# A separate VectorE side queue for layer 1's additions, served first

## The chip, the cores and the metric

The kernel runs on one core of a Trainium2 chip. The core has five engines that run their own instruction streams and meet at semaphores: PE (TensorE, matrix products), DVE (VectorE), ACT (ScalarE), POOL (GpSimd, here mostly an issuer of DMAs) and SP (SyncE, issues DMAs only). SBUF is the working memory, PSUM the small memory that PE writes its products to. The metric is the device time of one execution in microseconds (us). Several executions are timed and the median is given. The profile is one further execution, recorded by the hardware profiler.

## The reference

The input is x with 8 images of 32 channels and 128 x 128 pixels, in float32. Two layers follow each other, each adding its result to its input.

```
# layer 0: x = x + conv0(gn(x)), gn = group norm with 16 groups
xb   = patch_match_stack(g)          # per pixel the 8 best of 25 shifts, 32 -> 256 channels
dct  = conv(xb, dct_w, groups=32)
h    = relu(dw3x3(conv1x1(xb, w1), w2))
h    = relu(dw3x3(conv1x1(h,  w3), w4))
wien = sigmoid(dw3x3(conv1x1(h, w5), w6))
x    = x + conv1x1(conv(wien * dct, inv_dct_w, groups=32), agg_w)
# layer 1: x = x + conv1(gn(x)), one 5x5 kernel for every channel
x    = x + conv2d_5x5(gn(x), kernel, padding=2)
```

`patch_match_stack` sums squared differences between x and its 25 shifts over the channels, sums them over 3 x 3 pixels, takes the 8 smallest of the 25 for each pixel and gathers the shifted pixels.

## The kernel before

**The main loop.** Layer 0 of an image is worked off in steps of 8 rows: 16 steps and one for the edge, 17 per image, 136 in all, and two more to drain the pipeline. In each step the loop `for i in (3, 2, 1, 0)` makes four turns. Turns 3, 2 and 1 work on the three pairs of 1x1 and depthwise 3x3 convolutions, each for another row group, and turn 0 on the last multiplication and aggregation. So a row group that leaves stage 1 in one step enters stage 2 in the next. The 256 channels of each stage are split in two. The depthwise convolution of the first 128 channels runs on PE (L751, evicted by ACT at L764), that of the second 128 on DVE as eight multiply-adds over 128 x 1024 elements (L725, after a first tap by ACT at L722; the activation at L729 is ACT's too). The 1x1 products of PE are L670 (second half, evicted by ACT at L678) and L694 (first half, evicted by ACT at L701). L631 gathers pixels as a product with a selection matrix, which ACT makes at L616 and L617. In turn 0, PE makes L810 (`pc`), DVE multiplies it into the accumulators (L818), PE aggregates (L831, `pa`), and DVE adds the layer's input and takes statistics (L839, L840).

**Side work.** All that isn't in this pipeline is written as generators that say with `yield` on which queue they go on: "D" for DVE with a cost in us, "A" for DMAs and ACT, "P" and "Q" for PE. On D there are the squared differences of the next image (L444), their box sums (L508 to L520), the eight best (L536, L537), the places to gather from (L551 to L560) and layer 1 of the image that layer 0 has just finished. `push` (L211) lets a generator run to its next `yield` and appends it to that queue. `run` (L217) takes tasks from the front of a queue as long as the taken costs stay under a credit. In each turn, `tick` (L1017) serves D once: it adds a share of the image's side work to `owed` and gives `run("D", ...)` that credit. P is served before L810 in each turn, after L670 of the turn and after the L831 left over from the step before (`next(later)`); A is served once per turn, later. PE, DVE and ACT execute their instructions in the order in which the program wrote them, which these queues set.

**Layer 1** of an image works in four blocks of eight channels. `load` (L873) reads 8 channels from DRAM on POOL's queue. Then on D, DVE normalises them (L897, eight operations). On P, PE multiplies by the five bands of the 5x5 kernel (L924, `p5` in the program and `p` in the profile's names: 20 products into two PSUM tiles). On D again, DVE adds the two PSUM tiles to x (L936, two additions), POOL issues four DMAs of the result (L938), and the load of the next block goes to A. Four rows in the middle of the image that the two halves of the partitions can't reach are done by `middle` (L948: L959, L960 and 25 multiply-adds at L972). For the last image the additions carry a cost of 3.6 and include the next block's normalisation.

**PSUM.** The pool `ps_x` has five tiles, used by L631, L670, L694, L810, L831, L924 and others. A tile can be written again when its reader is through. The tiles of L924 are held until the additions at L936 have read them.

The text numbers layer 1's blocks of an image 0 to 3. "Image 0" is the first whose layer 1 runs, which is while layer 0 works on the next image.

Of the kernel before, what the change touches and what calls it, by code (L numbers as in the profile page):

```python
# [16 lines left out]
P = 128  # L17
# [27 lines left out]
def bm3d_conv_preact(  # L45
# [155 lines left out]

    queues = {"D": deque(), "A": deque(), "P": deque(), "Q": deque()}

    PAIR = 1.95
    pairs = [0]
# [3 lines left out]
    def push(task):  # L211
        want = next(task, None)
        if want:
            which, cost, *wait = want
            queues[which].append((cost, task, now[0] + (wait[0] if wait else 0)))

    def run(which, credit=1e9, limit=2):  # L217

        q, took = queues[which], 0.0
        for _ in range(len(q) if which != "D" else 1000):  # L220

            i = next(
                (
                    i
                    for i, (c, _, at) in enumerate(q)
                    if at <= now[0] and (c != PAIR or pairs[0] < limit)
                ),
                None,
            )
            if i is None or took >= credit:  # L230
                break
            cost, task, _ = q[i]
            del q[i]
            took += cost
            pairs[0] += cost == PAIR
            push(task)
        if which == "Q":
            pairs[0] = 0
        return took
# [8 lines left out]
    def group_stats(mv, name):  # L248

        lhsT = cst[:, C_G : C_G + P]  # L250
        mr = work.tile([P, 2], F32, name=f"mr_{name}", tag="mr")
        tmp = work.tile([P, 2], F32, name=f"tmp_{name}", tag="stmp")
        yield "P", 0
        pm = ps_x.tile([P, 512], F32, name=f"pm_{name}", tag="x")
        nc.tensor.matmul(pm[:, 0:1], lhsT, mv[:, 0:1], start=True, stop=True)
        nc.scalar.copy(mr[:, 0:1], pm[:, 0:1])
        yield "D", 0.3
        nc.vector.tensor_sub(tmp[:, 0:1], mv[:, 0:1], mr[:, 0:1])
        nc.vector.scalar_tensor_tensor(
            tmp[:, 1:2], tmp[:, 0:1], tmp[:, 0:1], mv[:, 1:2], op0=ALU.mult, op1=ALU.add  # L260
        )
        yield "P", 0
        pv = ps_x.tile([P, 512], F32, name=f"pv_{name}", tag="x")
        nc.tensor.matmul(pv[:, 0:1], lhsT, tmp[:, 1:2], start=True, stop=True)
        nc.scalar.copy(tmp[:, 0:1], pv[:, 0:1])
        yield "D", 0.2
        yield from inverse_std(mr[:, 1:2], tmp[:, 0:1], tmp[:, 0:1])
        return mr
# [579 lines left out]
    def layer1(b):  # L848

        yield "D", 0.2  # L850
        mv = work.tile([P, 2], F32, name=f"mv1_{b}", tag="mv1")
        nc.vector.bn_aggr(mv, stats[b].rearrange("p a b -> p (a b)"))
        mr = yield from group_stats(mv, f"b{b}")
        dg = work.tile([C, 2, C], F32, name=f"dg_{b}", tag="dg")
        for i in range(2):
            nc.vector.tensor_scalar(
                dg[:, i], ident[:C, :C], mr[:C, i : i + 1], None, op0=ALU.mult
            )
        yield "P", 0
        pb = ps_x.tile([P, 512], F32, name=f"pb_{b}", tag="x")  # L860
        nc.tensor.matmul(
            pb[:, : 2 * C], ones, dg.rearrange("p a b -> p (a b)"), start=True, stop=True
        )
        bc = work.tile([P, 2, C], F32, name=f"bc_{b}", tag="bc")
        nc.scalar.copy(bc.rearrange("p a b -> p (a b)"), pb[:, : 2 * C])
        last = b == NB - 1
        if last:
            ends = xnp.tile([P, HR, HX], F32, name="ends", tag="xn")
            ends = ends.rearrange("p r x -> p (r x)")[:, : 8 * 4 * W]
            ends = ends.rearrange("p (g c x) -> p g c x", g=8, x=W)  # L870
        xys = {}

        def load(c):  # L873


            if last:
                m = work.tile([P, 2, 4, W], F32, name=f"xo_{c}", tag="sel", bufs=4)
                t = [ends[:, c // 4], ends[:, c // 4 + 1], m[:, 0], m[:, 1]]
            else:
                t = [  # L880
                    work.tile([P, 4, W], F32, name=f"{name}_{b}_{c}_{e}", tag=name)
                    for name, e in (("xy", 0), ("xm", 0), ("xy", 1), ("xm", 1))
                ]
            src = x1d[b].rearrange("c y x -> y c x")
            nc.gpsimd.dma_start(t[0], src[:, c : c + 4])
            for h in range(2):
                nc.gpsimd.dma_start(
                    t[1][64 * h : 64 * h + 64], src[64 - 64 * h : P - 64 * h, c + 4 : c + 8]
                )
            nc.gpsimd.dma_start(t[2], src[:, c + 4 : c + 8])  # L890
            xys[c] = t

        def normalise(c):
            t = xys[c]
            for e in range(2):
                for i in range(4):
                    nc.vector.tensor_scalar(  # L897
                        t[3 - 2 * e][:, i],
                        t[e][:, i],
                        bc[:, 0, c + 4 * e + i : c + 4 * e + i + 1],  # L900
                        bc[:, 1, c + 4 * e + i : c + 4 * e + i + 1],
                        op0=ALU.subtract,
                        op1=ALU.mult,
                    )

        for c in range(0, C if last else 8, 8):
            load(c)
        push(middle(b, mr))
        for c in range(0, C, 8):
            if c == 0 or not last:  # L910
                yield "D", 2.0, 1 if last else 3
                normalise(c)
            yield "P", 0
            ps = [
                ps_x.tile([P, 4, W], F32, name=f"p5_{b}_{c}_{e}", tag="x") for e in range(2)
            ]
            t = xys.pop(c)

            for k, dx in enumerate((0, -2, -1, 1, 2)):
                xa, xz = max(0, -dx), min(W, W - dx)  # L920
                for h in range(2):
                    for e in range(2):
                        r, o = 64 * h, 64 * ((h + e) % 2)
                        nc.tensor.matmul(  # L924
                            ps[e][o : o + 64, :, xa:xz],
                            band[r : r + 64, dx + 2, r : r + 64],
                            t[3 - 2 * e][r : r + 64, :, xa + dx : xz + dx],
                            start=k == 0,
                            stop=k == 4,
                        )  # L930
            yield "D", 3.6 if last else 1.6
            if last and c + 8 < C:
                normalise(c + 8)
            for e in range(2):
                y = t[2 * e]
                nc.vector.tensor_add(y, y, ps[e])  # L936
                for a, z in ((0, 62), (66, P)):
                    nc.gpsimd.dma_start(  # L938
                        out[b, c + 4 * e : c + 4 * e + 4, a:z].rearrange("c y x -> y c x"),
                        y[a:z],  # L940
                    )
            if c + 8 < C and not last:
                yield "A", 0, 1
                load(c + 8)

        done.add((b, 0))
# [62 lines left out]
    def end(b, n, xr, j0, j1):  # L1009
        yield from final_add(b, n, accs.pop((3, b, n)), xr, j0, j1)  # L1010
        if n == NS:
            push(layer1(b))

    total = 5.5 + 3.3 + 36 * 1.95 + 4 * 4.6 + 32 * 1.85 + 4 * 2.6 + 4 * 3.6 + 6.6
    owed = [0.0]

    def tick(b, i):  # L1017

        now[0] += 1
        owed[0] += total / (NS - 2 if b else NS - 6) * (0.4 if i == 0 else 0.2)  # L1020
        owed[0] -= run("D", owed[0], 2 if i else 0) if owed[0] > 0 else 0
        owed[0] = min(owed[0], 6.0)

    def turn(credit):
        now[0] += 1
        run("D", credit)
        run("A")
        run("P")
        run("Q")

    def until(cond, credit):
        while not cond():
            turn(credit)

    with tc.manual_schedule(engines=ORDERED):
# [6 lines left out]
        for u in range(7):  # L1042
            unit(gather_load, u)

            for _ in range({2: 3, 3: 1}.get(u, 0)):
                turn(4.0)
            unit(gather_select, u - 2)
            unit(gather_pixels, u - 3)
# [6 lines left out]
        for s in range(len(steps) + 2):  # L1055
# [10 lines left out]
            for i in (3, 2, 1, 0):  # L1066
# [22 lines left out]
                if s < len(steps):  # L1089
                    unit(gather_select, u + 1, (0,))  # L1090
                    unit(gather_load, u + 3)
                    tick(b, i)
# [85 lines left out]
```

## Time and profile before

| | us |
|---|---|
| median of 3 runs | 6544.47 (6539.76 to 6554.23) |
| the profiled execution's own time | 6544.27 |
| its span, first to last instruction | 6542.5 |
| PE busy | 6179.8 (94%) |
| DVE busy | 5857.8 (90%) |
| ACT busy | 5058.6 (77%) |
| POOL busy | 3087.2 (47%) |
| layer 1's additions (L936) | 64 of 680 ns each |
| layer 1's products (L924) | 4.48 us for a block's 20 |

A row of the waits says which instruction stood idle until which other was through, with the total in us, how often, and the longest. A row of a timeline gives the start, the length, the engine, the line, what is written from what, and in brackets how long the engine was idle before and who released it. The mean clock granted to TensorE is 0.98 of full speed. Each DMA's issue is a row of its queue's engine.

### The profile page before, as it was taken

The numbers are of one execution on the slowest core, as the hardware profiler recorded it, in microseconds if no ns is written. First come the engines' busy times: TensorE is split into PE (matmuls) and PEld (weight loads), VectorE is DVE, ScalarE is ACT, GpSimd is POOL, SyncE is SP. The second block draws the span as 40 slices with busy tenths as digits, with TensorE's granted clock in tenths as the row PEclk, the third lists the DMA queues.
The fourth block names the chain that finished last, engine by engine and source line by source line (L and its number), as shares of the span: only waits on it lengthen the run. The fifth ranks groups of instructions, "written<-read, shape, count | busy, mean of one in ns | idle before, by whom it ended". The sixth has DMA issues, their size and how long they took to land.

```text
span 6542.5 us, 234200 instructions
## 1 busy us (share of the span) xinstructions
PE 6179.8 (94%) x102306; PEld 3215.9 (49%) x102306; DVE 5857.8 (90%) x8828; ACT 5058.6 (77%) x6698; POOL 3087.2 (47%) x5015
## 2 busy tenths in 40 slices
PE   4799999999999999999999999999999999999997
PEld 1444445455554545545454544544545454455553
DVE  7899988999989999999989999889998999878776
ACT  5787769778787877887788787977869788787772
POOL 8345436444364444644446444554345544334334
PEclk8899999999999999999999999999999999999998
DMA  4555555555555555565556555555555555455553
GB/s 85 126 134 144 125 126 143 141 143 138 131 149 138 137 146 129 145 151 134 140 132 156 136 137 141 134 142 140 139 135 134 146 146 138 115 147 144 136 134 81
DMA packets 544960, 886.21 MB, mean 135 GB/s; under 512 B 248880, under 2 KB 312944, under 8 KB 543936
## 3 DMA queue, kind: packets, MB, share of 16 engines
q0 software_dynamic: 383648, 611.87, 37.3%
q1 hardware_dynamic: 157776, 258.11, 16.1%
q8 instruction: 805, 13.19, 0.9%
q10 hardware_dynamic: 2512, 1.25, 0.1%
q14 instruction: 219, 1.79, 0.1%
HBM read 420.60 MB, written 216.49 MB: 97 GB/s over the span
## 4 chain that ended last, share of the span: by engine, by line
PE 55%; DVE 26%; POOL 5%; ACT 5%; DMA 4%; issue 4%; SPq 0%; ACTq 0%; DVEq 0%; POOLq 0%
PE pw L751 18%; DVE acc L725 17%; PE pv L670 14%; PE p L694 13%; PE pg L631 4%; POOL xtd L424 3%; DVE idx L537 3%; PE pc L810 2%; DMA t<-t 2%; DVE df L444 1%; PE pd L459 1%; PE p L924 1%; PE pa L831 1%; DVE acc L818 1%; ACT df L452 1%
## 5 line engine op out<-in xcount | busy, mean ns | idle before, releaser
L725 DVE SCALAR_TENSOR_TENSOR acc<-tv,dwv,acc 128x1024 f32<-128x1024 f32 (+3 forms) x3264 | 4032.1, 1237 | 163.7 <-ACT acc L722 59.9
L751 PE MATMUL pw<-t,dwd 96*32 96x254 f32 (+7 forms) x31680 | 2113.2, 419 | 23.8 <-DMA t<-t 17.9
L751 PEld LDWEIGHTS pw<-t,dwd 96*32 96x32 f32 (+1 forms) x31680 | 1079.9, 110 | 850.1 <-issue 385.5
L616 ACT ACTIVATE sel<-ib,nplace 128x1024 f32<-128x1024 uint8 x1024 | 1170.6, 1143 | 62.3 <-DMA ib<-idxd 62.3
L617 ACT ACTIVATE sel<-sel 128x1024 f32<-128x1024 f32 x1024 | 1086.0, 1061 | 32.5
L670 PE MATMUL pv<-acc,lw 128*32 128x512 f32 x8448 | 964.3, 593 | 49.9 <-DVE acc L818 41.7
L694 PE MATMUL p<-acc,lw 128*32 128x256 f32 x16768 | 977.4, 380 | 19.4 <-DVE xy L936 19.4
L602 POOL DMA_DIRECT2D ib<-idxd x512 | 293.0, 572 | 1209.2 <-ACT sel L616 1099.4
L791 POOL DMA_DIRECT2D xf<-xbd x1088 | 653.6, 633 | 329.2 <-PE pc L810 187.1
L694 PEld LDWEIGHTS p<-acc,lw 128*32 128x32 f32 x16768 | 568.0, 111 | 411.2 <-issue 59.3
L678 ACT COPY tv<-pv 128x512 f32<-128x512 f32 (+2 forms) x784 | 437.0, 578 | 366.9 <-PE pv L670 358.8
L729 ACT ACTIVATE acc<-acc 128x1024 f32<-128x1024 f32 (+3 forms) x408 | 417.3, 1023 | 349.0 <-DVE acc L725 348.8
L631 PE MATMUL pg<-sel,xt 120*32 120x88 f32 (+1 forms) x24576 | 609.9, 245 | 56.6 <-ACT sel L617 56.2
L631 PEld LDWEIGHTS pg<-sel,xt 120*32 120x32 f32 x24576 | 559.3, 111 | 211.5 <-ACT sel L617 72.2
L670 PEld LDWEIGHTS pv<-acc,lw 128*32 128x32 f32 x8448 | 289.1, 111 | 531.8 <-issue 414.6
L764 ACT ACTIVATE acc<-pw 128x512 f32<-128x512 f32 (+2 forms) x808 | 438.7, 573 | 143.6 <-PE pw L751 141.0
L444 DVE TENSOR_TENSOR df<-xn 128x786 f32<-128x786 f32 (+2 forms) x576 | 530.5, 973 | 1.0 <-PE pd L459 0.7
L701 ACT COPY t<-p 128x512 f32<-128x512 f32 x800 | 423.9, 572 | 137.5 <-PE p L694 137.5
L452 ACT ACTIVATE df<-df 128x786 f32<-128x786 f32 (+2 forms) x576 | 457.8, 859 | 40.8 <-DVE df L444 39.5
L722 ACT ACTIVATE acc<-tv,dwv 128x1024 f32<-128x1024 f32 (+3 forms) x408 | 455.1, 1115 | 44.1 <-PE pa L831 29.7
L694 PE MATMUL p<-xb,lw 128*32 128x256 f32 x8192 | 473.5, 383 | 14.4 <-DVE xy L936 14.4
L844 POOL DMA_DIRECT2D x1d<-xr x544 | 278.3, 518 | 417.9 <-DVE xr L839 300.8
(155 smaller groups left out, 6053.2 us busy)
## 6 DMA issues: line engine op xcount, KB each, us to landing
ib<-idxd POOLq DMA_DIRECT2D x512, 256.0 KB, 4.1
xbd<-xb POOLq DMA_DIRECT2D x128, 1024.0 KB, 6.0
xf<-xbd POOLq DMA_DIRECT2D x960, 128.0 KB, 6.8
t<-t SPq DMA_DIRECT2D x792, 128.0 KB
t<-t SPq DMA_DIRECT2D x384, 256.0 KB
tv<-tv SPq DMA_DIRECT2D x384, 130.0 KB
xt<-xtd POOLq DMA_DIRECT2D x240, 180.0 KB, 3.9
xtd<-xl POOLq DMA_DIRECT2D x192, 96.0 KB, 3.3
```

Source lines behind the costliest of these rows:

```text
L444: nc.vector.tensor_sub(df[:, :, ca:cz], xn[:, r0 : r0 + SR, ca:cz], xn[:, r0 + dy : r0 + dy + SR, ca + dx : cz + dx],)
L452: nc.scalar.activation(df[:, :, ca:cz], df[:, :, ca:cz], AF.Square)
L616: nc.scalar.activation(sel, ib, AF.Square, bias=nplace)
L617: nc.scalar.activation(sel, sel, AF.Relu, scale=-1.0, bias=1.0)
L631: nc.tensor.matmul(pg[C * j : C * (j + 1), :, :, xa:xz], xt[: 8 * QW, f * (NT // 2) + t], sels[j // 2][: 8 * QW, j % 2 * 2 : j % 2 * 2 + 2 ...
L670: nc.tensor.matmul(ps[C * j : C * (j + 1), :hr], lhsT[:, g, P + C * j : P + C * (j + 1)], src(g)[:, h : h + hr], start=g == 0, stop=g == 1,)
L694: nc.tensor.matmul(ps[C * r : C * (r + 1), e, :nb], lhsT[:, g, s], rows[:, r : r + 4 * nb - 3 : 4], start=g == 0, stop=g == 1,)
L722: nc.scalar.activation(acc, rows, AF.Copy, scale=tap)
L725: nc.vector.scalar_tensor_tensor(acc, rows, tap, acc, op0=ALU.mult, op1=ALU.add)
L751: nc.tensor.matmul(pt[u][C * j : C * (j + 1), ka:kz, :nb, xa:xz], dwd[0:hi, i - 1, u, j, dx + 1], t[0:hi, j, ka:kz, :nb, xa + dx : xz + dx ...
L764: nc.scalar.activation(rows[:, u : u + 2 * nh[u] - 1 : 2, :nb], pt[u][:, : nh[u], :nb], funcs[i - 1])
L791: nc.gpsimd.dma_start(xf[p : p + C, m, j0:j1], src[g, m, (h + m + 1) % 2, :, :, ya:yz])
```

## The change

A fifth queue, "B", is made. The additions of layer 1 (with the four output DMAs and the push of the next load that stand behind them) are put there instead of into D, except those of the last image, which stay in D. `tick` serves B before D, without a credit, and takes the cost of what it served from `owed`. `turn`, which is used outside the main loop, serves B before D as well.

```
-    queues = {"D": deque(), "A": deque(), "P": deque(), "Q": deque()}
+    queues = {"B": deque(), "D": deque(), "A": deque(), "P": deque(), "Q": deque()}
...
-            yield "D", 3.6 if last else 1.6
+            yield "D" if last else "B", 3.6 if last else 1.6
...
     def tick(b, i):
         now[0] += 1
+        owed[0] -= run("B")
         owed[0] += total / (NS - 2 if b else NS - 6) * (0.4 if i == 0 else 0.2)
         owed[0] -= run("D", owed[0], 2 if i else 0) if owed[0] > 0 else 0
...
     def turn(credit):
         now[0] += 1
+        run("B")
         run("D", credit)
```

More of the change, by code (lines that the diff above doesn't have):

```diff
@@ L198, in bm3d_conv_preact @@
     xtd, xbd, idxd, x1d, stats = {}, {}, {}, {}, {}
-    queues = {"D": deque(), "A": deque(), "P": deque(), "Q": deque()}
+    queues = {"B": deque(), "D": deque(), "A": deque(), "P": deque(), "Q": deque()}
     PAIR = 1.95
@@ L930, in layer1 @@
                         )
-            yield "D", 3.6 if last else 1.6
+            yield "D" if last else "B", 3.6 if last else 1.6
             if last and c + 8 < C:
@@ L1019, in tick @@
         now[0] += 1
+        owed[0] -= run("B")
         owed[0] += total / (NS - 2 if b else NS - 6) * (0.4 if i == 0 else 0.2)
@@ L1025, in turn @@
         now[0] += 1
+        run("B")
         run("D", credit)
```

## The prediction

> **What bounds the kernel now.** I read the page's busy shares first, then the waits of PE and DVE, then the timelines around layer 1's blocks.
>
> ```profile
> PE 6179.8 (94%) x102306; PEld 3215.9 (49%) x102306; DVE 5857.8 (90%) x8828; ACT 5058.6 (77%) x6698; POOL 3087.2 (47%) x5015
> PE 55%; DVE 26%; POOL 5%; ACT 5%; DMA 4%; issue 4%; SPq 0%; ACTq 0%; DVEq 0%; POOLq 0%
> ...
> PE pv L670 <- DVE acc L818: 41.7, 20, 3.7
> PE p L694 <- DVE xy L936: 33.7, 18, 3.6
> ...
> DVE xr L839 <- PE pa L831: 284.8, 75, 13.8
> DVE xy L936 <- PE p L924: 19.3, 9, 4.8
> ```
>
> PE and DVE are both nearly full, and the chain of waits passes between them. PE loses 33.7 us in 18 waits for layer 1's additions: the two tiles of L924 are two of the five PSUM tiles that L694 also draws on. DVE's largest idle time is a wait for PE.
>
> Image 0, block 0, DVE then PE:
>
> ```profile
> 1165.86 1.11 DVE L897 TENSOR_SCALAR xm<-xm,bc 128x128 f32<-128x128 f32 x4
> 1166.89 0.22 DVE L959 COPY mid<-mid 128x128 f32<-128x128 f32 x1
> ...
> 1174.20 10.52 DVE L725 SCALAR_TENSOR_TENSOR acc<-tv,dwv,acc 128x1024 f32<-128x1024 f32 x8
> ...
> 1186.29 1.27 DVE L936 TENSOR_TENSOR xy<-xy,p 128x512 f32<-128x512 f32 x2
> ...
> 1168.96 4.48 PE L924 MATMUL p<-xm,band 64*64 64x512 f32 x40
> ...
> 1187.02 3.19 PE L694 MATMUL p<-acc,lw 128*32 128x256 f32 x32 [3.21 <-DVE xy L936]
> ```
>
> The products end at 1173.44, the additions come 12.85 us later, and L694 waits 3.21 for them. But DVE isn't idle in between: other work fills the place where the additions will stand.
>
> The place that decides whether late DVE work costs time lies two to three steps after block 3:
>
> ```profile
> 1499.84 10.52 DVE L725 SCALAR_TENSOR_TENSOR acc<-tv,dwv,acc 128x1024 f32<-128x1024 f32 x8
> 1510.27 2.47 DVE L818 TENSOR_TENSOR acc<-acc,pc 128x512 f32<-128x512 f32 x4
> ...
> 1511.01 5.34 PE L670 MATMUL pv<-acc,lw 128*32 128x512 f32 x32 [2.21 <-DVE acc L818]
> ```
>
> From the input addition at 1470.39 to here DVE has no gap, and PE stands waiting for it. All DVE lateness left at 1470 reaches PE in full, and PE's own earliness is lost.
>
> **The change part by part.** No instruction is added or removed. In the changed program's order the 24 blocks of images 0 to 5 move (48 additions). In image 6 the side queue is empty and the order stays; the last image's additions stay in D. With each block go four output DMAs, and for three of four the next load's four DMAs, one turn earlier on POOL; the normalisations of blocks 2 and 3 and some squares shift too. The sum is made against the profiled execution (6544.3 us with a span of 6542.5; the median is 6544.5).
>
> The additions now come at the first tick after their products are written. DVE executes in order, so if PE isn't through, everything behind them waits. I lay image 0 out by its rows, with 680 ns per addition (1.2 us of DVE per block).
>
> *Block 0.* The additions follow the normalisation directly (end 1166.97). The products end at 1173.44: DVE stands 6.5 us. Behind it are the middle rows (4.7), L839/L840 (0.8), taps (10.4 per L725 group), and through them ACT's L729 and PE's L831. The first L818 then ends near 1219.5 instead of 1213.1. PE, without its 3.2 wait, is at its second L670 tile at 1216.2, whose PSUM tile that L818 must free: it waits 3.3, and L831 starts at 1221.4 against 1221.02. The 3.2 is given back: +0.4 on PE. ACT stands 6.4 for L729 at 1212.7, and catches up in its 15 us of waits for PE in that step.
>
> *Block 1.* The additions move from behind L818 to before the last taps; the products ended at 1248, so no DVE stall. L631 now takes a tile that the first addition frees, with DVE 5.6 late at 1254.3 against PE's 1252.4: +1.9. In return L810, which waited for L818 there (3.9 us for products that take 1.95 elsewhere), doesn't: -1.9. PE stays at +0.4. DVE's lag shrinks to 1.3 in the 3.63 idle before L839 at 1273.32 and smaller gaps.
>
> *Block 2.* Normalisation and products come one turn earlier, so that the products precede L810. They hold two of five tiles while L810 needs four: its fourth waits for the first L818, which stands behind taps and ends near 1313.0, with PE ready at 1310.9. PE: +2.2, together +2.6; minus the 0.43 wait that goes, +2.2. DVE's own 1.75 wait for the products goes, but L831 is later, so DVE gains nothing.
>
> *Block 3.* The products come after L831 (end 1368.79) and the additions directly after the normalisation (end 1365.04). Products until 1368.7+2.2+4.48=1375.4: DVE stands 10.3. PE's 2.63 wait goes, bringing it to about -0.4. From here the order is as before, and DVE's lag can only shrink in its idle times up to the second L839: 0.27+0.63+1.55+2.57+0.37=5.4. Left at 1470: 4.9 us, and PE takes it over at 1500 to 1511.
>
> *All six images.* Without PE's lateness the block-3 stalls are, by the same two rows in each image, 8.1, 7.7, 7.6, 7.6, 7.6 and 7.6 (46.2). Six times 2.2 add 13.2. DVE's idle times after them are 5.4, 4.9, 3.8, 3.1, 4.4 and 5.7 (27.3). Sum: 46.2+13.2-27.3=32 us. The 33.7 of removed waits are inside this: they precede the point at which DVE sets PE's time.
>
> Unknown sizes. PE's lateness at block 3: between 0 (19 us in all) and the longest wait of PE for L818, 3.7+0.4 (43 us); I take 2.2, worked out for the place itself. DVE's idle times: usable in full, or not at all where PE or ACT are late too (59 us); in full, as PE is about level there. POOL: a load or selection list that lands otherwise shows in PE's waits for ACT's selection (2.3 at the longest), plus or minus 14 over six images; nothing tells the sign, so 0. The middle rows, L840 and the squares change place within DVE's own time, already counted. SP's queue has none of the moved DMAs.
>
> A rule to weigh against this: PE's repeated 2 to 3 us gaps at L694 are rows of this trace. The Trainium skill, "Perfetto Trace Analysis", section "Optimization Strategy", says that a gap repeating on the engine that should be saturated can mean too little PSUM for the next tile. By that rule alone freeing the tiles earlier would return the 33.7 us (6510.6 us); by the rows above it gives 6576.
>
> **The rivals.** *DVE absorbs the stalls, PE keeps its gain:* 6544.3-33.7=6511 at best. For it: DVE idles 10% and waits 284.8 us for L831. Against: those waits lie mostly in other steps; in the steps behind the blocks it has 3 to 6 us. It decides if the block-3 stall stays under that idle time, and PE gains only if L818 isn't late at 1511 either; it was late by 2.21 before. *Even:* stalls of 7.6 without PE's lateness, and about 3 us more idle time per image than I count (18 in six), as in the best image against the worst: 46.2-27.3-18=1 us, 6545. For it: the idle times do differ by 2.6 us between images. *Much slower:* nothing is absorbed, and each block-0 stall leaves a rest as well: 59 and up to 6 times 6.5, 6604 to 6642. Against it: 3.63 idle in step 20, which eats block 0's rest.
>
> **How the numbers follow.** A measurement tells about 0.2% (13 us) from no change. Forecast, 6576 (with its bounds, about 6558 to 6604): 0.74. Even: 0.10. Faster: 0.07. Much slower: 0.09. Slower by over 0.2% is 0.74+0.09=0.83, within it 0.10, faster 0.07. The range 6552 to 6604 leaves out the last two and part of "even".
>
> **What would show it.** DVE's wait of L936 for L924 rises from 19.3 to about 107 us (per image 6.1 to 8.6 in block 0 and about 10 in block 3; block 2's go); L694's wait for L936 nearly goes; L810's and L631's waits for L818 and L936 appear in blocks 2 and 1. The distance between the input additions two steps after block 3 and block 0 of the same image grows by some 5 us in each of six images, and the rest of an image keeps its length. I'd be wrong if DVE's wait stays under 60 us, or if PE's wait for L818 near 1511 shrinks rather than grows.

## The result and the profile after

| | before | after |
|---|---|---|
| median, us | 6544.47 (6539.76 to 6554.23) | 6586.01 (6573.0 to 6596.13, 5 runs) |
| ratio to before | 1 | 1.0067, 95% interval 1.0054 to 1.0081 |
| profiled execution, us | 6544.27 | 6586.01 |
| its span, us | 6542.5 | 6584.2 |
| PE busy / the rest of the span, us | 6179.8 / 362.7 | 6199.5 / 384.7 |

The change makes the kernel slower, by 41.5 us in the medians and 41.7 in the profiled executions. The forecast was 6576, with a range of 6552 to 6604.

The page of the kernel after, its busy times and the shares of the chain that ended last:

```profile
PE 6199.5 (94%) x102306; PEld 3283.7 (50%) x102306; DVE 5860.7 (89%) x8828; ACT 5046.9 (77%) x6698; POOL 3076.1 (47%) x5015
...
PE 46%; DVE 34%; POOL 5%; ACT 5%; DMA 5%; issue 4%; SPq 0%; ACTq 0%; DVEq 0%; POOLq 0%
```

DVE's part of the chain went from 26% to 34%, though its busy time rose by 2.9 us only: the same instructions, but the end now hangs on them more often. PE is busy for 19.7 us longer with the same 102306 products; this comes back in the last section.

Two waits of the kernel before that rise (total us, times, longest):

```profile
PE pg L631 <- ACT sel L617: 56.2, 35, 2.3
...
PE pc L810 <- DVE acc L818: 5.9, 6, 1.4
```

The waits of PE and DVE in the kernel after:

```profile
PE pg L631 <- ACT sel L617: 73.2, 46, 2.3
PE pv L670 <- DVE acc L818: 70.1, 35, 3.6
...
PE pc L810 <- DVE acc L818: 9.9, 6, 2.1
...
PE pg L631 <- DVE xy L936: 2.0, 4, 1.5
...
DVE xr L839 <- PE pa L831: 243.1, 61, 10.0
DVE xy L936 <- PE p L924: 109.8, 14, 9.5
```

L694's 33.7 us of waiting for the additions are gone, as the queue frees the tiles earlier. In return the additions wait 90.5 us more for their products, PE waits 28.4 us more for L818 at L670, and L631 17.0 us more for ACT's selection. DVE gets 41.7 us back at L839.

DVE's timeline of the kernel after, at block 0 and block 3 of image 0:

```profile
1165.67 1.20 DVE L897 TENSOR_SCALAR xm<-xm,bc 128x128 f32<-128x128 f32 x4
1175.73 1.29 DVE L936 TENSOR_TENSOR xy<-xy,p 128x512 f32<-128x512 f32 x2 [8.86 <-PE p L924]
...
1379.28 1.29 DVE L936 TENSOR_TENSOR xy<-xy,p 128x512 f32<-128x512 f32 x2 [9.44 <-PE p L924]
```

PE's timeline of the kernel after, at the products of blocks 0 and 2 and the two places where a late L818 stops it:

```profile
1171.20 4.48 PE L924 MATMUL p<-xm,band 64*64 64x512 f32 x40
...
1222.50 3.64 PE L670 MATMUL pv<-acc,lw 128*32 128x512 f32 x16 [3.58 <-DVE acc L818]
...
1308.65 4.48 PE L924 MATMUL p<-xm,band 64*64 64x512 f32 x40
...
1315.72 1.08 PE L810 MATMUL pc<-xf,ldct 64*64 64x512 f32 x6 [0.88 <-DVE acc L818]
```

Both stalls stand where the prediction put them, directly behind the normalisation. DVE's 8.86 us at block 0 are followed by PE's 3.58 at L670, one step later: about the 3.2 us that PE had gained at L694, given back.

Where the time comes from is seen best in the input additions (L839), of which the first of each step is a clock of the kernel. The table gives how much later than in the kernel before they start, counted from the last input addition ahead of block 0 (1113.73 in image 0), as the mean of images 0 to 5, worked out from one execution's trace of each kernel. The columns name the steps by the time at which image 0 has them in the kernel before. The last column is what has gathered by the step in which image 6's block 0 runs.

| profiled kernel | 1173, behind block 0 | 1273, behind block 1 | 1323, behind block 2 | 1369, behind block 3's normalisation | 1423 | 1470 | all six images |
|---|---|---|---|---|---|---|---|
| after | 8.0 | 2.6 | 3.3 | 13.7 | 8.1 | 7.5 | 41.2 |
| after, block 3 a turn later | 7.1 | 1.8 | 2.1 | 3.8 | 2.2 | 2.2 | 6.3 |
| after, block 0 as before | -0.3 | -2.2 | -1.9 | 8.5 | 3.0 | 2.4 | 10.8 |
| both of these | -0.2 | -2.1 | -1.8 | -0.3 | -1.7 | -1.7 | -12.6 |
| block 0 alone | 7.4 | 8.4 | 8.1 | 8.2 | 8.9 | 8.8 | 48.4 |
| block 3 alone | -0.1 | -1.1 | -1.0 | -1.0 | -4.5 | -4.9 | -30.1 |
| behind the side work | 1.8 | -3.3 | -2.9 | 4.4 | -1.1 | -1.7 | -12.6 |
| second turn | -0.1 | 0.3 | -1.4 | 8.9 | 13.4 | 13.5 | 82.5 |

In the kernel after an image loses 3.3 us up to block 2 and 4.2 more (7.5 - 3.3) through block 3.

### The profile page after: what moved, and what is told of

It reads as the page before. It is cut to its first block, busy times and chain, and to the rows that moved or that the text cites. A ratio compares the mean times of both kernels' runs of the same rounds, so it can differ in the third digit from the quotient of the medians.

```text
span 6584.2 us, 234207 instructions
## 1 busy us (share of the span) xinstructions
PE 6199.5 (94%) x102306; PEld 3283.7 (50%) x102306; DVE 5860.7 (89%) x8828; ACT 5046.9 (77%) x6698; POOL 3076.1 (47%) x5015
## 3 DMA queue, kind: packets, MB, share of 16 engines
q10 hardware_dynamic: 2512, 1.25, 0.1%
## 4 chain that ended last, share of the span: by engine, by line
PE 46%; DVE 34%; POOL 5%; ACT 5%; DMA 5%; issue 4%; SPq 0%; ACTq 0%; DVEq 0%; POOLq 0%
DVE acc L725 22%; PE pw L751 15%; PE pv L670 12%; PE p L694 10%; PE pg L631 4%; DVE idx L537 3%; POOL xtd L424 3%; DVE df L444 2%; PE pc L810 2%; PE p L924 1%; DVE acc L818 1%; DVE mx L536 1%; ACT df L452 1%; PE pa L831 1%; ACT sel L616 1%
## 5 line engine op out<-in xcount | busy, mean ns | idle before, releaser
L751 PE MATMUL pw<-t,dwd 96*32 96x254 f32 (+7 forms) x31680 | 2124.9, 420 | 21.1 <-DMA t<-t 9.9
L751 PEld LDWEIGHTS pw<-t,dwd 96*32 96x32 f32 (+1 forms) x31680 | 1122.1, 111 | 817.1 <-issue 374.1
L670 PE MATMUL pv<-acc,lw 128*32 128x512 f32 x8448 | 966.7, 592 | 75.7 <-DVE acc L818 70.1
L694 PE MATMUL p<-acc,lw 128*32 128x256 f32 x16768 | 972.9, 379 | 0.0
L694 PEld LDWEIGHTS p<-acc,lw 128*32 128x32 f32 x16768 | 570.6, 111 | 392.5 <-issue 67.9
L631 PE MATMUL pg<-sel,xt 120*32 120x88 f32 (+1 forms) x24576 | 619.8, 245 | 77.1 <-ACT sel L617 73.2
L631 PEld LDWEIGHTS pg<-sel,xt 120*32 120x32 f32 x24576 | 564.9, 111 | 240.6 <-ACT sel L617 93.7
L670 PEld LDWEIGHTS pv<-acc,lw 128*32 128x32 f32 x8448 | 291.0, 110 | 555.6 <-issue 404.3
L694 PE MATMUL p<-xb,lw 128*32 128x256 f32 x8192 | 469.1, 380 | 0.0
L670 PE MATMUL pv<-xb,lw 128*32 128x512 f32 x4096 | 467.6, 594 | 0.0
```

The source lines that it names most:

```text
L631: nc.tensor.matmul(pg[C * j : C * (j + 1), :, :, xa:xz], xt[: 8 * QW, f * (NT // 2) + t], sels[j // 2][: 8 * QW, j % 2 * 2 : j % 2 * 2 + 2 ...
L670: nc.tensor.matmul(ps[C * j : C * (j + 1), :hr], lhsT[:, g, P + C * j : P + C * (j + 1)], src(g)[:, h : h + hr], start=g == 0, stop=g == 1,)
L694: nc.tensor.matmul(ps[C * r : C * (r + 1), e, :nb], lhsT[:, g, s], rows[:, r : r + 4 * nb - 3 : 4], start=g == 0, stop=g == 1,)
L751: nc.tensor.matmul(pt[u][C * j : C * (j + 1), ka:kz, :nb, xa:xz], dwd[0:hi, i - 1, u, j, dx + 1], t[0:hi, j, ka:kz, :nb, xa + dx : xz + dx ...
```

## The experiments

The theory was the prediction's: block 3's stall costs, block 0's is absorbed, and PE's removed waits are worth nothing by themselves. The rivals were that the removed waits are worth their length, that block 0's stall isn't absorbed, and that the queue's priority costs something whatever its stalls. All kernels below were timed beside the kernel before on the same chip; ratios are to it, with 95% intervals.

### One block at a time

Block 3 alone in the new queue:

```
-            yield "D" if last else "B", 3.6 if last else 1.6
+            yield "B" if c == 24 and not last else "D", 3.6 if last else 1.6
```

> Only block 3's additions go on the new queue. They then stand one turn earlier than before, behind the taps of the third stage, where by the rows of before the products have just ended (1381.0 against 1380.9): no stall over 0.3 us, and PE's wait for them (2.4 to 2.6 us per image, 14 in all) goes. Theory (DVE's position at the check point sets the time, so PE's waits ahead of it are worth nothing): 6540 to 6550. Rival B (each wait of PE that goes is gained): 6530. If even this costs 20 us or more, the stall isn't the cause.

Measured: 6520.39 us, ratio 0.9963 (0.9950 to 0.9977). Faster than before by 24 us: the theory, which left nothing to gain, missed it, and the gain is above rival B's 14 us too. The timelines of this kernel, image 0, DVE and then PE:

```profile
1380.90 1.28 DVE L936 TENSOR_TENSOR xy<-xy,p 128x512 f32<-128x512 f32 x2 [0.19 <-PE p L924]
...
1409.69 2.47 DVE L818 TENSOR_TENSOR acc<-acc,pc 128x512 f32<-128x512 f32 x4
...
1419.01 0.41 DVE L839 TENSOR_TENSOR xr<-xr,pa 128x256 f32<-128x256 f32 x1
...
1505.47 2.47 DVE L818 TENSOR_TENSOR acc<-acc,pc 128x512 f32<-128x512 f32 x4
...
1395.81 3.66 PE L694 MATMUL p<-xb,lw 128*32 128x256 f32 x64
```

The same stretch of the kernel before:

```profile
1397.96 1.27 DVE L936 TENSOR_TENSOR xy<-xy,p 128x512 f32<-128x512 f32 x2
...
1411.23 2.48 DVE L818 TENSOR_TENSOR acc<-acc,pc 128x512 f32<-128x512 f32 x4 [1.55 <-PE pc L810]
...
1423.26 0.42 DVE L839 TENSOR_TENSOR xr<-xr,pa 128x256 f32<-128x256 f32 x1 [2.57 <-PE pa L831]
...
1398.69 5.35 PE L694 MATMUL p<-xb,lw 128*32 128x256 f32 x64 [2.63 <-DVE xy L936]
```

With the other blocks in D, block 3's products come behind L670, as in the kernel before, and not directly behind L831 as in the kernel after, and the additions stand behind a group of taps: they find their products all but ready (0.19 us). PE isn't held up at L694, where it waited 2.63 us and then took 5.35 us for the same 64 products instead of 3.66 (the last section comes back to this), and so is earlier at L810 and L831. DVE's two waits for PE, 1.55 and 2.57 us, go, and L818 at the point that decides runs at 1505.47 where it ran at 1510.27. The prediction had counted these idle times only as room to absorb lateness; they are also time that PE can give back to DVE. That the removed waits are worth nothing has fallen.

Block 0 alone:

```
-            yield "D" if last else "B", 3.6 if last else 1.6
+            yield "B" if c == 0 and not last else "D", 3.6 if last else 1.6
```

> Only block 0's additions go on the new queue: the stall of DVE in block 0 (6 to 9 us per image) stays, while blocks 1 to 3 stand as before. Theory of the prediction: DVE's idle time in the next two steps (about 5 us, then 5.7 us) takes the lag up, PE's 3 us are given back: 6540 to 6550. Rival C (block 0's lag survives to the check point by what goes beyond the first 5 us, as in the profile of the changed kernel, whose lag at the third input addition behind block 0 is about 4 us): 6555 to 6570.

Measured: 6599.84 us, ratio 1.0085 (1.0071 to 1.0099): slower than the whole change, and above both expectations. Nothing of the absorption that the theory had is seen. PE's timeline of this kernel, behind block 0 and in block 1:

```profile
1220.42 2.87 PE L670 MATMUL pv<-acc,lw 128*32 128x512 f32 x16 [3.55 <-DVE acc L818]
...
1267.40 1.98 PE L810 MATMUL pc<-xf,ldct 64*64 64x512 f32 x6 [4.50 <-DVE acc L818]
```

Block 1's two tiles are still held at 1267, so L810 needs one that the late L818 frees, and PE takes over DVE's lateness there. The 3.63 us of idle time before L839, which were to absorb it, exist only if PE is on time; here L839 comes 9.6 us late in image 0, after 5.09 us of waiting for PE. In the kernel after, block 1's tiles are free by then, and the lag shrinks from 8.0 to 2.6 us.

### The two stalls against each other

Four kernels make a square: block 0's stall there or not, block 3's there or not, with blocks 1 and 2 early in all of them, as in the kernel after. What it prices is a block's place at the head of the queue as a whole, the stall less the wait of PE that goes with it, not the stall alone. Block 0 as before, the others in the queue:

```
-            yield "D" if last else "B", 3.6 if last else 1.6
+            yield "B" if c and not last else "D", 3.6 if last else 1.6
```

> The changed order for blocks 1, 2 and 3 of images 0 to 5; only block 0's additions stay where they were before. If block 0's stall is what costs in the changed kernel (its rest passes into PE), this lies near or below the kernel before: 6525 to 6555 us, with block 3's stall of 8 to 9 us still there in each image (some 50 us of DVE's wait in all) and mostly absorbed or paid for by PE's removed wait. If, as the prediction had it, block 3's stall is the loss and block 0's is absorbed, most of the loss stays: 6565 to 6590 us.

The kernel after, with block 3's additions one turn later:

```
-            yield "D" if last else "B", 3.6 if last else 1.6
+            yield "D" if last else "B", 3.6 if last else 1.6, 2 if c == 24 and not last else 0
```

> The changed kernel with only block 3's additions one turn later (behind layer 3's taps, where they found their products done elsewhere); block 0 keeps its stall. If block 0's stall carries the loss, little changes: 6570 to 6590 us with DVE's wait for L924 falling from 110 to some 55 us. If the prediction's block-3 term is right (46.2 + 13.2 - 27.3 us), all of the loss goes and the time is 6540 to 6555 us. Between, each carries a part.

Both of these edits:

```
-            yield "D" if last else "B", 3.6 if last else 1.6
+            yield "B" if c and not last else "D", 3.6 if last else 1.6, 2 if c == 24 and not last else 0
```

> Only blocks 1 and 2 come as early as in the changed kernel; block 0 as before, block 3 one turn later so that it finds its products done. Without any stall at the head of DVE: 6515 to 6540 us, DVE's wait for L924 below 15 us. If the earlier blocks 1 and 2 are themselves what costs 13 us in the kernel without block 0, it stays at 6550 to 6562 us.

| | block 3's stall | no stall in block 3 |
|---|---|---|
| block 0's stall | 1.0067 (1.0054 to 1.0081), 6586.01 us | 1.0035 (1.0021 to 1.0049), 6569.75 us |
| block 0 as before | 1.0019 (1.0010 to 1.0028), 6557.86 us | 0.9989 (0.9980 to 0.9998), 6536.46 us |

The waits of DVE in the kernel with block 3 later:

```profile
DVE xy L936 <- PE p L924: 53.7, 8, 9.5
```

and in the one with block 0 as before:

```profile
DVE xy L936 <- PE p L924: 58.5, 9, 9.0
```

The two stalls have about half of the 109.8 us each. Block 0's place costs 0.48% in the one column and 0.46% in the other, some 31 us, and block 3's 0.32% and 0.30%, some 20 us; each difference is known to between 0.13% and 0.19%, and within this the two add up. So each carries a part, as the last sentence of the second expectation had it. That block 0's is the larger rests on 1.0035 against 1.0019, whose intervals overlap. The kernel with block 3 later is at the lower end of what the theory of block 0 gave, the one with block 0 as before 3 us above its upper end. (The profiled execution of the kernel with block 3 later was its shortest, 6550.25 us, so its row in the table above is some 3 us per image too small.)

The kernel without either stall is inside its first expectation (DVE's wait is 6.1 us) and a little faster than before, but slower than block 3 alone, by 0.26%: with blocks 1 and 2 a turn earlier PE waits 10.8 us at L670 for the additions and 19.6 at L751 for SP's copies, where it waits 0 and 9.6 in the kernel with block 3 alone. That these waits are the whole of it was not tried.

### The queue kept, the stalls taken away

The same queue with the same priority, but what is taken from it in a tick is written behind the tick's other side work:

```
         now[0] += 1
         owed[0] += total / (NS - 2 if b else NS - 6) * (0.4 if i == 0 else 0.2)
+        early = [queues["B"].popleft()] if queues["B"] else []
+        owed[0] -= sum(e[0] for e in early)
         owed[0] -= run("D", owed[0], 2 if i else 0) if owed[0] > 0 else 0
+        for e in early:
+            push(e[1])
```

> The additions stay on their own queue and in the same turn as in the changed kernel, but stand behind the side work of that turn instead of ahead of it. So PE's products get 4.7 us (block 0: the middle rows) and 3.6 us (block 3: four squares) more before DVE needs them. Theory (DVE stands still at the head of the turn, and what is left of that lag at the check point behind block 3 is what an image loses): the waits of DVE for L924 fall from 110 us to about 45 (block 0 some 3 us, block 3 some 5 us per image), the lag at the check point falls from about 7 to 0 to 2 us per image, time 6545 to 6557. Rival A (the cost comes from the turn itself: the PSUM tiles of block 2 being held while L810 needs four, and the next load going out a turn earlier): both are as in the changed kernel, so 6580 to 6590.

Measured: 6526.93 us, ratio 0.9968 (0.9958 to 0.9979); 59 us faster than the kernel after, by an order in which only the middle rows, the places to gather from and four squares per image have changed sides with the additions. Block 0 in DVE's timeline:

```profile
1167.47 3.85 DVE L972 SCALAR_TENSOR_TENSOR mid<-mid,kb 128x128 f32<-128x128 f32 x10
1172.21 1.28 DVE L936 TENSOR_TENSOR xy<-xy,p 128x512 f32<-128x512 f32 x2 [0.89 <-PE p L924]
```

Some 5 us of middle rows fill most of the time in which the products are made, and 0.89 us of the stall are left in image 0 (16.0 in six images, against 47.1 in the kernel after). So the queue by itself isn't what costs. The expectations missed that this is a gain: PE keeps its 3.2 us at L694, and the table shows 3.3 us won per image behind block 1. Block 3's remaining stall (7.57 us in image 0) then costs 7.3 us, of which 5.5 have come back by 1423. Made a turn later for block 3 as well:

```
-            yield "D" if last else "B", 3.6 if last else 1.6
+            yield "D" if last else "B", 3.6 if last else 1.6, 2 if c == 24 and not last else 0
...
-        early = [queues["B"].popleft()] if queues["B"] else []
+        ready = queues["B"] and queues["B"][0][2] <= now[0]
+        early = [queues["B"].popleft()] if ready else []
```

> As the kernel whose additions come behind the side work of the same tick, and block 3's wait one turn more, so that they stand behind layer 3's taps. If the queue's priority is worth something once no addition stands at the head of DVE before its products are done, the 7.6 us of stall in block 3 go as well and the time falls below that kernel's 6527 and that of block 3 alone (6520): 6495 to 6520 us, DVE's wait for L924 under 25 us. If the gains of the two don't add, because both remove the same wait of PE, it stays at 6518 to 6530 us. If a later block 3 holds the two tiles longer than it helps, 6530 us or more.

Measured: 6524.19 us, ratio 0.9974 (0.9964 to 0.9984), DVE's wait for L924 14.3 us. Block 3's stall is gone, but the time is within the first version's interval: L694 waits for the additions again (12.0 us, 6 times). The second expectation's time held; that the gains don't add because both take away the same wait of PE fits with this, but wasn't shown apart.

The other way to avoid stalls is to be later. Served first, but not before the second turn:

```
-            yield "D" if last else "B", 3.6 if last else 1.6
+            yield "D" if last else "B", 3.6 if last else 1.6, 0 if last else 2
```

> The queue of its own, served first, as in the changed kernel; but the additions may come only at the second turn after their products are issued. If the loss comes from waiting at the head of DVE and not from the queue, the stall of DVE for L924 falls to below 30 us and the time is 6515 to 6545 us. If it comes from the side work that is pushed back by the additions, the stall goes but the time stays at 6565 us or more.

Measured: 6623.78 us, ratio 1.0123 (1.0108 to 1.0139), the slowest of all, though no addition of images 0 to 5 waits for its products. PE's timeline of this kernel, image 0, and its waits in all:

```profile
1261.64 1.98 PE L810 MATMUL pc<-xf,ldct 64*64 64x512 f32 x6 [3.03 <-DVE acc L818]
...
1337.10 3.64 PE L670 MATMUL pv<-acc,lw 128*32 128x512 f32 x16 [4.75 <-DVE xy L936]
...
1424.29 1.98 PE L810 MATMUL pc<-xf,ldct 64*64 64x512 f32 x6 [5.46 <-DVE acc L818]
...
PE pc L810 <- DVE acc L818: 47.2, 12, 5.5
...
PE pv L670 <- DVE xy L936: 39.2, 8, 6.8
```

Blocks 2 and 3 slip by a turn or more, and their tiles are held across L670 and L810. The time is above the second expectation's 6565 us, but its reason, the side work pushed back, isn't what the waits show: PE stands without tiles, 47.2 us at L810 (5.9 before) and 39.2 at L670 (none before), waits of the kind that the queue had removed at L694. Both ends of one scale are seen: additions too early stop DVE, additions too late stop PE.

Last, blocks 0 and 3 together, with the tick of the first kernel of this section. Block 0's additions stand behind the tick's side work as there; block 3's are in the tick of the kernel with block 3 alone, but behind its four box sums and not ahead of them:

```
-            yield "D" if last else "B", 3.6 if last else 1.6
+            yield "B" if c in (0, 24) and not last else "D", 3.6 if last else 1.6
```

> Block 0's additions behind the side work of the same tick (stall of some 1 to 4 us instead of 7.9) and block 3's one turn before where they were; blocks 1 and 2 as before. If block 0's earlier place is worth PE's 3.2 us at L694 once it costs no stall, this falls below the kernel with block 3 alone (6520): 6500 to 6515 us. If the rest of that stall passes into PE at L810 in block 1, as it did with block 0 alone, the gain is eaten: 6520 to 6545 us.

Measured: 6536.87 us, ratio 0.9987 (0.9977 to 0.9996), as the second expectation had it. The waits of PE say why the gains don't add:

```profile
PE pc L810 <- DVE acc L818: 24.9, 6, 4.5
```

With block 1 in its old place L810 waits 4.5 us once in each image, as with block 0 alone (24.7 us there, 5.9 before). So the version with block 3 alone remains the fastest found (0.9963); the first one behind the side work (0.9968) can't be told from it.

### A stall taken out with its data

To price the stall with the order unchanged, the additions of images 0 to 6 read only their own tile, which leaves layer 1's convolution out of their results:

```
-                nc.vector.tensor_add(y, y, ps[e])
+                nc.vector.tensor_add(y, y, ps[e] if last else y)
```

> Changed kernel, but in all images except the last the additions at L936 add x to itself in SBUF instead of adding PSUM's tiles: the order on every engine stays, DVE just has nothing to wait for, and the PSUM tiles are free when the products are through. The convolution of layer 1 is left out of those images' results. Theory (waiting for L924 makes the cost): it vanishes, and since PE's waits for the additions are gone as well, the time falls below that of before, to 6500 to 6530. Rival A's load a turn earlier, the shifted squares and the DMA order are all still there: if they make the cost, it stays at 6570 or more.

Measured: 6548.01 us, ratio 1.0005 (0.9996 to 1.0015), between all expectations. The stalls of images 0 to 6 are gone and nearly all of the 41.5 us with them, but nothing is won below before. PE's timeline shows a wait that has come up:

```profile
1194.73 5.32 PE L751 MATMUL pw<-t,dwd 96*32 96x256 f32 x48 [6.68 <-DMA t<-t]
```

It stands for 56.6 us in 21 waits of L751 for SP's copies (17.9 before). SP's own rows just before it are long, 3.18 us for an issue that takes 0.55 at this place in the kernel before:

```profile
1180.63 3.18 SPq L707 DMA_DIRECT2D t<-t  x1
1183.86 1.66 SPq L709 DMA_DIRECT2D t<-t  x1
```

They follow 8 us behind the block's output DMAs (1172.80). Two kernels asked what delays the copies. First the loads of the next block two turns later (against the kernel just told):

```
-                yield "A", 0, 1
+                yield "A", 0, 3
                 load(c + 8)
...
-                yield "D", 2.0, 1 if last else 3
+                yield "D", 2.0, 1 if last or c else 3
                 normalise(c)
```

> The kernel whose additions don't read their products (layer 1's convolution is left out of images 0 to 6), and in which the loads of blocks 1 to 3 are issued two turns later. If PE's new wait of L751 for SP's copies (56.6 us, 21 times) comes from these loads running beside the copies, it falls below 25 us and the time to 6500 to 6535 us. If the output DMAs or something else cause it, it stays above 45 us and the time at 6540 us or more.

Measured: 6550.83 us, ratio 1.0007 (0.9997 to 1.0017), and L751's wait 60.5 us. The loads aren't it. Then also the output DMAs two turns later, with the loads behind them (`store` issues one tile's two outputs, against the kernel with the late loads):

```
...
+            if not last:
+                yield "A", 0, 2
+                for e in range(2):
+                    store(c, e, t[2 * e])
             if c + 8 < C and not last:
-                yield "A", 0, 3
+                yield "A", 0, 1
                 load(c + 8)
```

> The kernel whose additions don't read their products (layer 1's convolution left out of images 0 to 6), with a block's output DMAs two turns later and the next load behind them. If the wait of L751 for SP's copies (60.5 us with the loads alone moved) comes from the output DMAs that are issued just before the copies, it falls below 30 us, and the time to 6500 to 6535 us. If PE only finds itself earlier at L751 than the copies can be, it stays above 45 us, whatever the output DMAs do, and the time at 6540 us or more.

Measured: 6572.86 us, ratio 1.0038 (1.0024 to 1.0053), the wait 86.9 us. It has moved: L751 at 1187 doesn't wait any more, and the long wait of image 0 now is in block 1's step, where the outputs are issued from 1249.47 on. PE's row:

```profile
1267.80 5.32 PE L751 MATMUL pw<-t,dwd 96*32 96x256 f32 x48 [7.12 <-DMA t<-t]
```

and SP's rows before it:

```profile
1256.89 2.43 SPq L707 DMA_DIRECT2D t<-t  x1
1259.37 2.29 SPq L709 DMA_DIRECT2D t<-t  x1
```

By its total the second expectation was right. By its place the first is nearer, as the wait has left block 0's step and stands in block 1's, behind that block's outputs; but behind block 0's outputs, which now start at 1182.04, PE doesn't wait. What makes the copies slow is open, and so this group doesn't give a price of DVE's stall by itself; the square above gives that of a block's place.

## Why the prediction was right, and where it wasn't

The direction and nearly the size were right: +32 us forecast, +41.5 measured, and most of the signs that it named came: L936's wait at 109.8 us (about 107 forecast), L694's wait gone, new waits of L810 in block 2 and of L631 for the additions, and 7.5 us per image up to two steps behind block 3, counted as in the table, where some 5 were forecast. One sign didn't come, and it was one of the two that were to show the prediction wrong: PE's wait for L818 near 1511 was to grow. It is 2.20 us against 2.21 in image 0, and over images 0 to 5 it shrank from 13.2 to 8.6 us. PE's timeline of the kernel after shows why, the same L670 in three steps one behind the other:

```profile
1423.58 3.64 PE L670 MATMUL pv<-acc,lw 128*32 128x512 f32 x32 [0.78 <-DVE acc L818]
...
1470.03 3.64 PE L670 MATMUL pv<-acc,lw 128*32 128x512 f32 x32 [1.42 <-DVE acc L818]
...
1519.14 3.64 PE L670 MATMUL pv<-acc,lw 128*32 128x512 f32 x32 [2.20 <-DVE acc L818]
```

In the kernel before only the third of them waits. So PE did take over DVE's lateness, but one and two steps earlier than the prediction had it. What the sum was made of was only half right, and that it came so near is in part luck:

**Block 0.** The first half of the step held: DVE's stall was followed by PE's wait at L670, 3.3 us forecast and 3.58 measured. The stall was 8.86 us in image 0 instead of 6.5, where PE comes to the products at 1171.20 instead of 1168.96, behind a stretch from 1149.6 on with its clock at one half; in six images it was 47.1 instead of the 41.4 that the prediction's rows give. What failed is "DVE's lag shrinks to 1.3 in the 3.63 idle before L839 at 1273.32": it is 5.0 there in image 0 and 2.6 in the mean. And PE, which the prediction left at +0.4, is later as well: counted as in the table, its L831 starts 2.6 us later in the step behind block 0 (1221.02 before), and 4.7 ahead of block 3's products, where the sum takes 2.2. The sum therefore has no term for block 0's stall, and the square shows some 31 us for block 0's place. The rival "much slower" had named this rest, and the idle time in step 20 was held against it.

**Block 2.** PE's +2.2 at L810 was too much: the wait is 0.88 us in image 0 (9.9 in six, with 5.9 at L810 in block 1 gone), and the lag grows by 0.6 us per image there. 13.2 us of the sum rest on it. PE's lateness at block 3 is there, and larger, but most of it comes from block 0.

**Block 3.** The stalls are 9.44 us in image 0 (10.3 forecast) and 52.3 in six (59.4 = 46.2 + 13.2 forecast). Of 52.3, 20 are left by the square, 25 (six times 4.2) by the table; forecast were all 32. So the idle times took up some 27 to 32 us, against 27.3 forecast. The bound that the prediction gave for a PE that isn't late, 46.2 - 27.3 = 19, fits the square's 20 in the kernel with block 0 as before, whose L831 ahead of block 3's products is 0.5 us early. With the 4.7 measured in the kernel after in place of 2.2, the prediction's own sum gives 46.2 + 28.2 - 27.3 = 47 us, where 41 to 42 were measured.

**Put at nothing.** For PE's waits for ACT's selection (L631) the prediction took 0, as nothing told the sign. They cost 17.0 us more, and they go with the stalls: 63.2 us with block 3 later, 67.4 with block 0 as before, 55.8 with neither, 56.2 before. And in image 6 the order didn't stay: block 0's additions move ahead of the middle rows and wait 9.46 us instead of 4.79, without a cost, as the lag is 41 us ahead of them and still 41 at the last input addition.

**PE's removed waits.** "The 33.7 us of removed waits are inside this" was refuted by block 3 alone: where the wait of L694 goes without a stall, 24 us are won. The error is the statement that DVE has no gap from 1470 to 1511 and so PE's earliness is lost; true as it is, DVE's place at 1470 was itself set by PE at 1411 and 1423. By the square, the prediction's block-0 and block-3 errors hide each other: a missing loss of 31 us, and 12 us too much in block 3, with 7 us won by the kernel without either stall (32 + 31 - 12 - 7 = 44, which is the 0.67%; by the medians it is 41.5).

**The rule.** The Trainium skill, "Perfetto Trace Analysis", section "Optimization Strategy", says that a repeated gap can mean too little PSUM, and the prediction set this against the rows. This change, which frees the tiles as early as it can, measured 1.0067 and not the 6510.6 us worked out by the rule. But tiles freed earlier without a stall gave 0.9963. So the gap was worth closing; the price was in how the additions were made early.

**The clock.** Not in the sum at all was that PE's work itself gets slower (the last section): of the 41.7 us between the two profiled executions 19.7 are busy time of PE and 22.0 the rest.

## What to carry to other kernels

A consumer put first in an in-order queue isn't early if its producer is still at work: it stops everything behind it, so give it a place by when its input is ready and put work of that length in front. An engine's idle time absorbs another's lateness only while the engine that it waits for is on time; check each shared tile in between, since a wait there hands the lateness on, and also look whether an idle time is itself the echo of the wait that you remove. Move one block at a time: the whole change lost 0.67%, and one quarter of it, in a place where nothing waits, gained 0.37%.

## What the runs showed of the hardware

A gap of PE can cost more than its length. Windows of the kernel after around the wait of 3.58 us at 1222.50 (start and end, length, then the busy time of PE, of its weight loads, DVE, ACT and POOL, the granted TensorE clock, the DMA share and GB/s):

```profile
1218.00:1222.00 4.00, 0.92 (x10) 0.01 (x2) 3.93 (x4) 0.12 (x1) 0.00 (x0) 0.92 0.70 184
1222.00:1226.00 4.00, 3.50 (x20) 0.88 (x24) 3.86 (x17) 3.97 (x6) 0.00 (x0) 0.50 0.06 19
1226.00:1230.00 4.00, 4.00 (x60) 2.04 (x56) 3.72 (x18) 3.04 (x5) 1.99 (x5) 0.73 0.03 8
```

And of the kernel whose additions don't read their products, around its 6.68 us at 1194.73:

```profile
1188.00:1192.00 4.00, 0.05 (x4) 0.00 (x0) 3.89 (x4) 3.07 (x4) 1.73 (x3) 0.87 0.84 211
1192.00:1196.00 4.00, 1.27 (x13) 0.70 (x17) 3.89 (x4) 0.00 (x0) 2.38 (x5) 0.50 0.90 203
1196.00:1200.00 4.00, 4.00 (x44) 2.23 (x40) 3.79 (x8) 0.60 (x1) 1.05 (x2) 0.50 0.26 61
1200.00:1204.00 4.00, 4.00 (x39) 1.14 (x35) 1.47 (x5) 1.18 (x2) 0.00 (x0) 0.85 0.30 85
```

Behind the gap the clock is at one half for a while, and the products that run then take up to twice as long: 48 of L751 take 5.32 us in the second kernel and 2.77 just before the gap. The clock's record in the traces has only 0.5 and 1.0; at 0.5 it stays mostly for 3.4 us (34 of 50 stretches in the kernel after, 11 more are of 6.8). Counted from 250 us on, with a fall inside a gap of PE or up to 2 us behind it, the clock of the kernel after fell at 1 of 38 gaps of 0.75 to 1.25 us, at 22 of 40 of 1.75 to 2.25 and at 14 of 15 of 3.25 or more (kernel before: 0 of 33, 13 of 27, 12 of 13). So it isn't the same each time: behind the wait of 2.21 us at 1511 the clock fell in the kernel before (0.60 in the 4 us from 1512 on, L670 in 5.34 us instead of 3.64), and behind the wait of 2.20 at 1519 in the kernel after it didn't.

The Trainium skill, "TensorE: Matmul & The Clock Gate", section "Why this matters for your kernels", advises against idle gaps of PE over some 3 us between bursts, since the clock then falls back. The runs agree on what happens, but here gaps of about 2 us were enough in half of the cases (22 of 40, 13 of 27).

With this, PE's busy time mostly moves the way that the whole time moves, with the same instructions. All profiled kernels, one execution of each, in us against before:

| profiled kernel | span | PE busy | rest |
|---|---|---|---|
| second turn | +93.2 | +38.5 | +54.7 |
| block 0 alone | +48.1 | +16.8 | +31.3 |
| after | +41.7 | +19.7 | +22.0 |
| additions that don't read, outputs and loads later | +30.9 | +6.0 | +24.9 |
| after, block 0 as before | +15.5 | +3.9 | +11.6 |
| additions that don't read, loads later | +11.9 | +3.3 | +8.6 |
| additions that don't read | +6.8 | +2.0 | +4.8 |
| after, block 3 a turn later | +5.9 | -2.4 | +8.3 |
| after, block 0 as before and block 3 a turn later | -12.2 | -3.6 | -8.6 |
| blocks 0 and 3 behind the side work | -15.0 | +0.7 | -15.7 |
| behind the side work | -15.9 | -2.5 | -13.4 |
| behind the side work, block 3 a turn later | -21.7 | -11.7 | -10.0 |
| block 3 alone | -32.2 | -10.5 | -21.7 |

Where the span differs by over 20 us, a fifth to a half of the difference is PE's busy time; of the smaller differences two have it with the other sign. So who prices a wait of PE by its length alone leaves a part out, and it isn't a fixed one. No kernel here changed the clock with the waits unchanged, so the split is read from the traces and not shown by an experiment.
